# Cross-attention with 16 batches: the last 128 key columns by 15 block products in column tiles, between the steps of the product with V

## The chip, the cores and the metric

The kernel runs on one core of a Trainium2 chip. The metric is device microseconds of one execution. Three runs of the kernel before took 944.00, 943.75 and 945.24 us, median 944.0. Engines go by short names: PE is TensorE (matrix products; PEld is its weight loading), DVE is VectorE, ACT is ScalarE, POOL is GpSimd, SP is SyncE, which starts most DMA transfers. PSUM is the memory that PE writes to, in banks of 512 float32 numbers per partition; SBUF is the working memory. Everything is float32, and each product that the program issues is carried out as two passes.

## The reference, cut to what matters

```python
# x: (16, 100, 640), context: (16, 722, 384); 8 heads of 80 columns
enc, ca = context[:, :718], context[:, 718:]          # 718 keys, 4 extra tokens
hs = mha(x @ Wq, enc @ Wk, enc @ Wv)                  # softmax over the 718 keys
q1 = einsum('btc,th->bch', ca, Wq_ca)[:, picked]      # 100 of 384 rows
hs1 = mha(q1, x, x)                                   # softmax over 100 keys
hs2 = mha(hs1 @ Wq, ca @ Wk_ca, ca @ Wv_ca)           # softmax over 4 keys
out = (hs + hs2) @ Wout + b_out + x
```

There are two larger attentions per batch: the main one over 718 keys, and a second one whose own softmax is over 100 keys (with a third, tiny one behind it).

## The kernel before, in words

The 718 keys of a batch are cut into three thirds u of 240 columns (KT), two of which share a column each with a neighbour, and each third into two blocks of up to 120 (KN). So there are six key blocks. The 640 columns of K and V are cut into chunks of 128 for K (HC = 5) and two halves for V.

The products `enc @ Wk` and `enc @ Wv` are, per batch, 3 x 2 results (a third u, a half g) of a product over three context chunks. Instead of 18 block products they are formed by 15, in the manner of the fast 3x3 by 3x2 schemes: sums of context blocks (`enc_sums`, on POOL, once per batch) times sums of weight blocks (`weight_sums`, once). `V_PLAN` and `K_PLAN` list, for each of the 15, a chain (a PSUM bank A to E in which products pile up), the number of the product, and the result (u, g) to which the bank's content at that moment is added. After each product the bank is read: copied where the result is new (by ACT), else added to it by DVE. The class `Blocks` does this; `Values` is V's, `Keys` is that of the first four chunks of K.

The fifth chunk of K (columns 512 to 640) has no partner chunk, and is formed in the plain way by `last_keys`: 9 products with 128x128 weights (`wk4`) and 240 moving columns (three thirds by three context chunks), one after the other, and two copies to `kT` by ACT.

Inside the batch loop the program's order is the order on every engine: each engine works through its own queue in the order in which the kernel's text issues, and waits on semaphores where data or a buffer is not ready. For a batch b the order on PE is: the scores of b (`scores`, three pairs of key blocks), small products of the second attention (`softmax2`, `products`), V of b and the four chunks of K of b+1 in turn (`both`, lines 440 and 471), the fifth chunk of b+1 (`last_keys`, line 565), the output projection of earlier rows where a block of 128 rows is complete (`project`, line 951; in no batch 0, 1, 5, 9, 13), the queries of the next two batches where b is odd (`queries`, line 541), and the product with V of b (line 1317). That last product goes in two halves g of four heads. Each half has 24 items (head h, key block i); each item is two products with 64 and 36 of the 100 query rows as weight columns, which lie in the two column tiles of 64 of the PE array, and 81 moving columns.

On DVE the running maximum of the scores and its handling (`Maximum`) precede the subtractions from the scores (line 1144) and ACT's exponentials (line 1152). `Maximum` has five steps, taken one by one with `go(n)`: a transpose of 32x32 blocks (672), a reduction (674), four and two or four small reductions (677, 684), a spread over 800 columns (694 on ACT for the main attention, 699 on DVE for the second), and a transpose back (702). `softmax1` runs these steps for the second attention of batch b+1, then subtracts (798); `exponentials1` (801) is ACT's exponential of it. In the kernel before, for batches from 1, `softmax1` stands behind the last subtraction, as a whole, and `exponentials1` before the product with V; in batch 0 four steps stand there, and the fifth and the exponential behind the product with V. After each half of the product with V DVE normalises (reciprocal 1329, multiplication 1331, and from batch 1 the sum with the second attention, 1338).

PSUM banks come from three pools of two: `ps2` (pairs of banks: V's chains A and B, two thirds of the scores, `last_keys`, `project`), `psk` (K's chains A and B, and every other small one) and `ps1` (the other chains, `a_ps` of the product with V). A tile is handed out in rotation when its former readers are done. Remaining raw context blocks (`rest`, line of `load_rest`) are loaded into a single buffer after their last readers.

Of the kernel before, what the change touches and what calls it, by code (L numbers as in the profile page):

```python
# [75 lines left out]
def load_packed(load, to, w):  # L76
# [38 lines left out]
    ("B", 14, (0, 0)),  # L115
    ("A", 5, (1, 1)),
]

K_PLAN = [V_PLAN[k] for k in (0, 1, 2, 3, 4, 6, 5, 7, 9, 11, 8, 12, 10, 13, 14)]

# [12 lines left out]
def kernel(  # L133
# [123 lines left out]

    wv_sb = const.tile([P, NF, H // 2], F32, name="wv_sb")
    wk_sb = const.tile([P, NF, 2, P], F32, name="wk_sb")
    wk4 = const.tile([P, CC, P], F32, name="wk4")  # L260
    wq_sb = const.tile([P, HC, H], F32, name="wq_sb")
    kT = const.tile([P, HC, 3, KT], F32, name="kT")
    wout_sb = const.tile([P, HC, H], F32, name="wout_sb")
# [100 lines left out]
    e1 = const.tile([P, ROWS], F32, name="e1")  # L364
    nc.gpsimd.memset(e1[96:, :], LOW)

    ys = []
    for j in range(2):
        y = const.tile([S, NH, HT + 1], F32, name=f"y_{j}")
        nc.gpsimd.memset(y[:, :, HT:], 1.0)  # L370
        ys.append(y)


    def first_values(i, enc, engines, halves=(0, 1), get=psum):
# [215 lines left out]
    def last_keys(b, enc):  # L590
        banks = pair(f"kT_ps_{b}")
        return chunk_keys(
            HC - 1,
            [banks[:, k] for k in range(2)],
            [wk4[:, c] for c in range(CC)],
            enc,
        )


    def scores(b, g, tiles):  # L600
# [124 lines left out]
    class Second:  # L725


        def __init__(self, b, xT, ca=None):
            self.b, self.xT = b, xT[:, b % 2]
            self.top = None  # L730

            self.ca = ca
            if ca is not None:
                return
            self.ca = small.tile([S, T, S], F32, tag="ca", name=f"ca_{b}", bufs=2)
            nc.sync.dma_start(
                out=self.ca, in_=cas[b].unsqueeze(0).to_broadcast([S, T, S])
            )
# [23 lines left out]
            return summed  # L762

        def copy(self):
            b, y_ps = self.b, self.y_ps
            self.y = ys[b % 2]
            nc.scalar.copy(
                self.y[:, :, :HT].rearrange("p (u h) k -> p u h k", u=2),
                y_ps[:S, HT : 11 * HT].rearrange("p (u h k) -> p u h k", u=2, h=5)[
                    :, :, :4, :  # L770
                ],
            )
# [19 lines left out]
        def softmax1(self, n=8):  # L792

            if not self.top:
                self.top = Maximum(e1, f"1_{self.b}")
            self.top.go(n)
            if self.top.over is not None:
                nc.vector.tensor_tensor(e1[:S], e1[:S], self.top.over[:S], ALU.subtract)

        def exponentials1(self):  # L800
# [255 lines left out]
    for c in range(HC):  # L1056
        w_ps = psum(f"w_ps_{c}")
        for cc in range(CC):
            nc.tensor.transpose(
                w_ps[:, cc * P : (cc + 1) * P], wkt_sb[:, c, cc * P : (cc + 1) * P], ident  # L1060
            )
        act(
            wk_sb[:, c % 2 : 6 : 2, c // 2] if c < HC - 1 else wk4,
            w_ps[:, : CC * P].rearrange("p (a n) -> p a n", a=CC),
        )

# [15 lines left out]
        weight_sums(nc.vector, wk_sb, False)  # L1082
    first_keys(enc)
    weight_sums(nc.vector, wk_sb, True)

    va = wide("va")[:, : H // 2]
    va_ps = psum("va_ps")
# [34 lines left out]
    for b in range(B):  # L1122
# [59 lines left out]
        if b == 0:  # L1182
            second.scores1()
            m_next = load_m(b + 2)
            kk.go(3)
            top.go(3)
            first_values(3, e_in, (act, act), get=bank)
            top.go(1)
            kk.go(2)
            now.scores2()  # L1190
            first_values(0, e_in, (act, act), (0,), bank)
            top.go()
            kk.go(3)
            first_values(0, e_in, (act, act), (1,), bank)
            now.softmax3()
            kk.go(2)
            subtract(0)
            exponential(0)
            kk.go(2)
            subtract(1)  # L1200
            kk.go(3)
            exponential(1)
            second_next, enc_next = loads()
            less = subtract(2)
            exponential(2)
            last_keys(b + 1, enc)
            enc_next = load_rest(b + 2, enc_next)
            keys(m_next)
            now.values2(less)
            enc_sums(enc_next)  # L1210
            second.softmax1(4)
        elif b + 1 < B:
            if b > 1:
                last.transpose()
            vv = Values(b, e_in)

            def both(n):
                vv.go(n)
                kk.go(n)

            second.scores1(seen)
            if b == 1:
                now.load()
            last.load()
            top.go(3)
            both(3)
            now.scores2()
            top.go(1)
            both(2)
            if b == 1:  # L1230
                nc.vector.tensor_tensor(last.hs[:S], last.hs[:S], last.hs2, ALU.add)
            top.go()
            both(2)
            if b == 1:
                last.transpose(get=psum1)
            both(1)
            now.softmax3()
            now.values2()
            vv.go(2)
            kk.go(1)  # L1240
            subtract(0)
            exponential(0)
            vv.go(1)
            subtract(1)
            vv.go(1)
            kk.go(2)
            exponential(1)
            vv.go(1)
            kk.go(2)
            both(1)  # L1250
            both(1)
            if b == 1:
                for f in list(wv_there):
                    nc.scalar.copy(wv_sb[:, W_AT[f]], wv_there.pop(f))
            second.load()
            if b == 1:
                nc.gpsimd.dma_start(out=bias, in_=bout[0].partition_broadcast(P))
            second_next, enc_next = loads()
            if b + 2 < B:
                m_next = load_m(b + 2)  # L1260
            subtract(2)
            exponential(2)
            last_keys(b + 1, enc)
            if b + 2 < B:
                enc_next = load_rest(b + 2, enc_next)
            second.softmax1()
            last.project()
        else:
            room = enc_tile("spare").rearrange("p f k -> p (f k)")
            spare.extend(room[:, i * H : (i + 1) * H] for i in range(2))  # L1270
            last.transpose()
            vv = Values(b, e_in)
            last.load()
            mine.load()
            top.go(3)
            vv.go(3)
            last.project_few(len(OC) - 2)
            now.scores2()
            top.go(1)
            vv.go(2)  # L1280
            top.go()
            vv.go(3)
            now.softmax3()
            now.values2()
            vv.go(2)
            subtract(0)
            exponential(0)
            vv.go(5)
            for i in (1, 2):
                subtract(i)  # L1290
                exponential(i)
            last.project()
# [3 lines left out]
        if b % 2 and b + 1 < B:  # L1296
            xT, tiles = xT_at[0], queries_tiles(p + 1)
            for n in range(HC):
                queries(p + 1, xT, tiles, n)
        if 0 < b < B - 1:  # L1300
            second.exponentials1()

        mine.hs = hs = hs_tile(f"hs_{b}")
        hs2 = now.hs2
        for g in range(2):
            a_ps = psum1(f"a_ps_{b}_{g}")
            a_v = a_ps[:S, : 4 * (D + 1)].rearrange("p (h e) -> p h e", e=D + 1)

            order = [(h, i) for h in range(4 * g, 4 * g + 4) for i in range(len(KC))]
            if g == 0:  # L1310
                order.sort(key=lambda at: at[1] // 2)
            for h, i in order:
                if b == B - 1 and h == NH - 1 and i == 0:

                    mine.transpose([(0, 2)])
                for lo, hi in QC:
                    nc.tensor.matmul(  # L1317
                        a_v[lo:hi, h % 4],
                        st[i // 2][: KEYS[i], i % 2, h * S + lo : h * S + hi],
                        block(i, h // 4)[: KEYS[i], h % 4],  # L1320
                        start=(i == 0 and h in (0, *range(4, NH))),
                        stop=(i == len(KC) - 1),
                        skip_group_check=True,
                    )
            if b == 0 and g == 1:
                second.softmax1()
                second.exponentials1()
            rs = small.tile([S, 4], F32, tag="rs", name=f"rs_{b}_{g}")
            nc.vector.reciprocal(rs.unsqueeze(2), a_v[:, :, D : D + 1])  # L1329
            cols = slice(4 * g * D, 4 * (g + 1) * D)  # L1330
            nc.vector.tensor_tensor(
                hs[:S, cols].rearrange("p (h d) -> p h d", h=4),
                a_v[:, :, :D],
                rs.unsqueeze(2).to_broadcast([S, 4, D]),
                ALU.mult,
            )
            if b:
                nc.vector.tensor_tensor(hs[:S, cols], hs[:S, cols], hs2[:, cols], ALU.add)
# [57 lines left out]
```

## Time and profile before

| what | value |
|---|---|
| median of the runs | 944.0 us |
| profiled execution: span | 942.4 us |
| PE busy | 934.5 us (99%) |
| DVE busy | 674.0 us (72%) |
| POOL busy | 623.1 us (66%) |
| ACT busy | 364.7 us (39%) |
| product with V, line 1317 | 3072 passes, 111.9 us |
| last and first key chunks by `chunk_keys`, line 565 | 7.7% of the chain that ended last |
| DVE waiting for the product with V (line 1329) | 111.0 us in 30 waits |

The time of the profiled execution itself is known by its span, 1.6 us below the median of the runs. Busy times of engines overlap; only the chain of work that ended last adds up to the span. A line of the timeline gives the start and the duration in microseconds, the engine, the line of the kernel, the operation, the tile written and the tiles read, shapes (partitions x elements), and, in brackets, how long the engine sat idle before it and what ended that. A matmul's own duration (366 ns for a pass of 240 columns) contains the way through the array; the next pass starts earlier.

### The profile page before, as it was taken

What the parts mean: (1) busy time and instruction counts of PE and PEld (TensorE: products, weight loads), DVE (VectorE), ACT (ScalarE), POOL (GpSimd) and SP (SyncE); (2) the same over time, 40 slices, a digit from 0 to 9 for tenths busy, and PEclk for the clock granted to TensorE, in tenths of its full rate; (3) what the DMA queues carried; (4) which work ended last, traced back from release to release, by engine and by line L of the source; (5) the groups of instructions that cost most, each with busy time, mean ns of one, the idle gap of its engine ahead of it and who ended that gap; (6) DMA issues with size and microseconds to landing.
All of it is one profiled execution on the core that took longest, in us unless ns stands there. A gap on an engine that the chain in (4) does not pass through costs nothing.

```text
span 942.4 us, 25629 instructions
## 1 busy us (share of the span) xinstructions
PE 934.5 (99%) x11215; PEld 796.2 (84%) x11215; DVE 674.0 (72%) x1084; ACT 364.7 (39%) x605; POOL 623.1 (66%) x565
## 2 busy tenths in 40 slices
PE   9999999999999999999999999999999999999998
PEld 6998979888797888989789887987989888897866
DVE  3559794977929688595955959578693886949684
ACT  1244443524334244433424334244431534334241
POOL 5857976776738757495873948657694576748514
PEclk9999999999999999999999999999999999999999
DMA  8822024040310404003050130403113030210300
GB/s 264 296 60 87 3 70 128 1 130 3 94 60 1 117 2 135 5 11 122 1 151 3 37 82 1 139 1 95 38 40 113 1 112 7 59 53 1 95 8 29
DMA packets 45367, 62.48 MB, mean 66 GB/s; under 512 B 13448, under 2 KB 37320, under 8 KB 43656
## 3 DMA queue, kind: packets, MB, share of 16 engines
q1 hardware_dynamic: 41720, 42.97, 15.2%
q0 software_dynamic: 2512, 16.72, 6.1%
q8 instruction: 88, 1.44, 0.6%
q10 hardware_dynamic: 1024, 1.15, 0.4%
q14 instruction: 23, 0.19, 0.1%
HBM read 55.26 MB, written 5.57 MB: 65 GB/s over the span
## 4 chain that ended last, share of the span: by engine, by line
PE 96%; DVE 3%; issue 0%; DMA 0%; ACT 0%; POOL 0%; ACTq 0%; DVEq 0%
PE s_ps L620 12%; PE a_ps L1317 12%; PE v_psA L440 10%; PE v_psB L440 8%; PE kT_ps L565 8%; PE k_psA L471 7%; PE q_ps L541 7%; PE o_ps L951 7%; PE k_psB L471 6%; PE v_psC L440 3%; PE k_psC L471 3%; PE y_ps L746 2%; PE v_ps L381 2%; PE v_psD L440 2%; PE v_psE L440 2%; PE k_psE L471 1%
## 5 line engine op out<-in xcount | busy, mean ns | idle before, releaser
L781 POOL TENSOR_TENSOR e<-ca,g 100x800 f32<-100x800 f32 x64 | 99.8, 1570 | 145.2 <-DVE most L1156 125.0
L870 POOL TENSOR_TENSOR hs<-vb,p 100x640 f32<-100x640 f32 x64 | 105.6, 1659 | 45.9 <-DVE p L856 32.5
L877 POOL TENSOR_TENSOR hs<-hs,hs 100x640 f32<-100x640 f32 x48 | 113.9, 2373 | 3.8
L1317 PEld LDWEIGHTS a_ps<-vs,st 120*36 120x36 f32 (+3 forms) x3072 | 109.1, 125 | 5.6 <-issue 5.5
L1317 PE MATMUL a_ps<-vs,st 120*36 120x81 f32 (+3 forms) x3072 | 111.9, 233 | 0.0
L440 PE MATMUL v_psA<-wv_sb,enc 128*120 128x320 f32 x352 | 109.5, 434 | 0.0
L506 POOL TENSOR_TENSOR enc<-enc 128x240 f32<-128x240 f32 x135 | 98.1, 736 | 16.9 <-DMA enc<-in_enct 9.8
L1144 DVE TENSOR_TENSOR st<-st,over 120x1600 f32<-120x1600 f32 x48 | 107.6, 2243 | 0.0
L637 ACT COPY st<-s_ps 120x800 f32<-120x800 f32 x64 | 49.7, 829 | 135.6 <-PE s_ps L620 135.6
L620 PE MATMUL s_ps<-qp,kT 32*120 32x100 f32 x3072 | 97.4, 263 | 0.0
L620 PEld LDWEIGHTS s_ps<-qp,kT 32*120 32x120 f32 x3072 | 94.7, 179 | 1.6 <-issue 0.2
L788 POOL TENSOR_TENSOR e<-e,e 100x800 f32<-100x800 f32 x48 | 90.4, 1884 | 3.8
L440 PE MATMUL v_psB<-wv_sb,enc 128*120 128x320 f32 x296 | 91.9, 433 | 0.0
L471 PE MATMUL k_psA<-enc,wk_sb 128*128 128x240 f32 x360 | 87.6, 366 | 0.0
L1329 DVE RECIPROCAL rs<-a_ps 100x4 f32<-100x4 f32 x32 | 5.8, 182 | 111.0 <-PE a_ps L1317 111.0
L1156 DVE TENSOR_TENSOR most<-most,st 120x800 f32<-120x800 f32 x64 | 66.2, 1034 | 24.1 <-ACT st L631 23.0
L1152 ACT ACTIVATE st<-st 120x1600 f32<-120x1600 f32 x48 | 73.9, 1539 | 22.3 <-DVE st L1144 22.2
L471 PEld LDWEIGHTS k_psA<-enc,wk_sb 128*128 128x128 f32 x360 | 68.2, 190 | 16.8 <-DVE kT L411 0.2
L440 PEld LDWEIGHTS v_psA<-wv_sb,enc 128*120 128x120 f32 x352 | 63.2, 183 | 22.6 <-issue 0.5
L471 PE MATMUL k_psB<-enc,wk_sb 128*128 128x240 f32 x300 | 73.1, 366 | 0.3 <-DVE sm L853 0.3
L440 PEld LDWEIGHTS v_psB<-wv_sb,enc 128*120 128x120 f32 x296 | 54.0, 183 | 21.9 <-DVE vs L411 0.4
L541 PE MATMUL q_ps<-xT,wq_sb 128*128 128x200 f32 x400 | 69.1, 333 | 0.0
(146 smaller groups left out, 1732.8 us busy)
## 6 DMA issues: line engine op xcount, KB each, us to landing
vb<-va_d POOLq DMA_DIRECT2D x16, 1000.0 KB, 7.4
enc<-in_enct SPq DMA_DIRECT2D x30, 240.0 KB, 3.9
enc<-in_enct SPq DMA_DIRECT2D x15, 360.0 KB, 3.6
xT<-in_xt SPq DMA_DIRECT2D x8, 500.0 KB, 4.3
rest<-in_enct SPq DMA_DIRECT2D x31, 120.0 KB, 6.6
xn<-in_x SPq DMA_DIRECT2D x11, 320.0 KB, 5.7
out<-xn SPq DMA_DIRECT2D x11, 320.0 KB, 3.2
ca<-in_cas SPq DMA_DIRECT2D x16, 156.2 KB
```

What stands on the lines that cost most here:

```text
L440: nc.tensor.matmul(at[0][j][:KN, : H // 2], a_form(self.enc, f)[:, j * KN : (j + 1) * KN], wv_there.get(f, wv_sb[:, W_AT[f]]), start=first ...
L471: nc.tensor.matmul(at[:, i * KT : (i + 1) * KT], wk_sb[:, W_AT[f], i], a_form(self.enc, f), start=(first and i == 0), stop=last, skip_grou ...
L506: nc.gpsimd.tensor_tensor(out, left, right, op)
L541: nc.tensor.matmul(q_ps[:, : 2 * S].rearrange("p (j s) -> p j s", j=2), wq_sb[:, c, n * P : (n + 1) * P], xT[:, :, c, :], start=(c == 0), ...
L565: nc.tensor.matmul(bank[:, i * KT : (i + 1) * KT], weights[c], a_raw(enc, u, c), start=(i == 0 and c == 0), stop=(c == CC - 1), skip_group ...
L620: nc.tensor.matmul(s_ps[r][:n, 256 * a + lo : 256 * a + hi], kT[rows, c, u, j * KN : (j + 1) * KN], rhs, start=(a == 0 and c == 0), stop=( ...
L781: first = nc.gpsimd.tensor_tensor(to, self.ca[:, t, :].unsqueeze(1).to_broadcast([S, NH, S]), g[:, :, t].unsqueeze(2).to_broadcast([S, NH, ...
L788: nc.gpsimd.tensor_tensor(e, e, to, ALU.add)
L870: first = nc.gpsimd.tensor_tensor(to, vb[:S, t, :].rearrange("p (h d) -> p h d", h=NH), p2[:, :, t].unsqueeze(2).to_broadcast([S, NH, D]), ...
L877: nc.gpsimd.tensor_tensor(sums, sums, to, ALU.add)
L1144: return nc.vector.tensor_tensor(st[i], st[i], top.over[:KN].unsqueeze(1).to_broadcast([KN, 2, ROWS]), ALU.subtract,)
L1317: nc.tensor.matmul(a_v[lo:hi, h % 4], st[i // 2][: KEYS[i], i % 2, h * S + lo : h * S + hi], block(i, h // 4)[: KEYS[i], h % 4], start=(i ...
```

## The change

The fifth chunk of K of batch b+1 is no longer formed by 9 full products. It is formed by the same 15 block products as the others, on weight blocks of 128x64 (`wk5`, with its own sums), by a new class `LastKeys`. `REST_PLAN` puts them into eight steps: seven with two products at a time, one in partitions 0 to 63 of one PSUM bank (chains A, D and E) and one in partitions 64 to 127 of another (chains B and C), that is in the two column tiles of 64; the last step is one product, cut into two halves of 120 columns. After each step each bank's new content is read: added by DVE where the result was begun, else copied, by ACT from the first bank and by DVE from the second.

The steps are placed inside the product with V: one before the items 1, 7, 13 and 19 of each half. In batches from 1 the second attention's `softmax1` is cut: two steps of it where it stood, and one after each of the first three key steps (small reductions; spread; transpose back with the subtraction). `exponentials1` now stands behind the second half of the product with V. In batch 0 the five steps stay where they were. Apart from that, the second attention's `y` has one tile instead of two, and batch 0's first keys still go by `last_keys`, with six of `wk5`'s blocks as weights.

```diff
+REST_PLAN = [
+    (("A", 7, (2, 1)), ("B", 13, (1, 0))),
+    (("A", 3, (2, 0)), ("C", 12, (0, 1))),
+    (("A", 9, (1, 0)), ("B", 8, (2, 0))),
+    (("A", 2, (0, 0)), ("B", 10, (2, 1))),
+    (("A", 0, (0, 1)), ("B", 4, (0, 1))),
+    (("A", 5, (1, 1)), ("B", 14, (0, 0))),
+    (("D", 1, (2, 0)), ("C", 11, (2, 1))),
+    (("E", 6, (1, 0)),),
+]
+REST_COLS = {"A": 0, "B": 0, "C": KT, "D": KT}
...
-    wk4 = const.tile([P, CC, P], F32, name="wk4")
+    wk5 = const.tile([P, NF, P // 2], F32, name="wk5")
...
+    class LastKeys:
...
+        def product(self, half, f, lo, cols, keys, first):
+            nc.tensor.matmul(
+                self.banks[half][64 * half : 64 * half + 64, lo : lo + cols],
+                wk5[:, W_AT[f]],
+                a_form(self.enc, f)[:, keys : keys + cols],
+                start=first,
+                stop=True,
+                skip_group_check=True,
+            )
+
+        def read(self, half, to, lo, cols, keys):
+            u, g = to
+            out = kT[64 * g : 64 * g + 64, HC - 1, u, keys : keys + cols]
+            left = self.banks[half][64 * half : 64 * half + 64, lo : lo + cols]
+            if to in self.begun:
+                nc.vector.tensor_tensor(out, left, out, ALU.add)
+            elif half:
+                nc.vector.tensor_copy(out, left)
+            else:
+                nc.scalar.copy(out, left)
+
+        def go(self, n=1):
+            for _, step in zip(range(n), self.steps):
+                begins = self.banks is None
+                if begins:
+                    self.banks = [psumk(f"k5_ps_{self.b}_{k}") for k in range(2)]
+                if len(step) == 1:
+                    ((_, f, to),) = step
+                    for half in range(2):
+                        self.product(half, f, 0, KN, half * KN, True)
+                    for half in range(2):
+                        self.read(half, to, 0, KN, half * KN)
+                    continue
+                for half, (chain, f, _) in enumerate(step):
+                    self.product(half, f, REST_COLS[chain], KT, 0, begins)
+                for half, (chain, _, to) in enumerate(step):
+                    self.read(half, to, REST_COLS[chain], KT, 0)
+                    self.begun.add(to)
...
-            self.y = ys[b % 2]
+            self.y = y_sb
...
-            if self.top.over is not None:
+            if self.top.over is not None and not self.less:
+                self.less = True
                 nc.vector.tensor_tensor(e1[:S], e1[:S], self.top.over[:S], ALU.subtract)
...
+    weight_sums(nc.vector, wk5)
...
-            last_keys(b + 1, enc)
             enc_next = load_rest(b + 2, enc_next)
...
-            last_keys(b + 1, enc)
             if b + 2 < B:
                 enc_next = load_rest(b + 2, enc_next)
-            second.softmax1()
+            second.softmax1(2)
             last.project()
...
-        if 0 < b < B - 1:
-            second.exponentials1()
+        k5 = LastKeys(b + 1, enc) if b + 1 < B else None
...
-            for h, i in order:
+            for at, (h, i) in enumerate(order):
+                if k5 and at % 6 == 1:
+                    k5.go()
+                    if b and at < 19:
+                        second.softmax1(1)
...
-            if b == 0 and g == 1:
-                second.softmax1()
+            if k5 and g == 1:
+                if b == 0:
+                    second.softmax1()
                 second.exponentials1()
```

More of the change, by code (lines that the diff above doesn't have):

```diff
@@ L365 @@
     nc.gpsimd.memset(e1[96:, :], LOW)
[L367 to L371, printed above, removed]
+    y_sb = const.tile([S, NH, HT + 1], F32, name="y_sb")
+    nc.gpsimd.memset(y_sb[:, :, HT:], 1.0)
     def first_values(i, enc, engines, halves=(0, 1), get=psum):
@@ L594, in last_keys, with __init__ @@
             [banks[:, k] for k in range(2)],
-            [wk4[:, c] for c in range(CC)],
-            enc,
-        )
+            [
+                wk5[:, 2 * c : 2 * c + 2].rearrange("p g n -> p (g n)")
+                for c in range(CC)
+            ],
+            enc,
+        )
+    class LastKeys:
+        def __init__(self, b, enc):
+            self.b, self.enc = b, enc
+            self.banks, self.begun = None, set()
+            self.steps = iter(REST_PLAN)
+        def product(self, half, f, lo, cols, keys, first):
[34 more added lines that the diff above has]
+                    self.begun.add(to)
     def scores(b, g, tiles):
@@ L729, in __init__ @@
             self.b, self.xT = b, xT[:, b % 2]
-            self.top = None
+            self.top, self.less = None, False
             self.ca = ca
@@ L764, in copy @@
         def copy(self):
-            b, y_ps = self.b, self.y_ps
-            self.y = ys[b % 2]
+            y_ps = self.y_ps
+            self.y = y_sb
             nc.scalar.copy(
@@ L1062 @@
         act(
-            wk_sb[:, c % 2 : 6 : 2, c // 2] if c < HC - 1 else wk4,
+            wk_sb[:, c % 2 : 6 : 2, c // 2]
+            if c < HC - 1
+            else wk5[:, :6].rearrange("p (a g) n -> p a (g n)", a=CC),
             w_ps[:, : CC * P].rearrange("p (a n) -> p a n", a=CC),
```

## The prediction

> **What bounds the kernel now.** I read the page's busy shares, the granted clock and the chain of work that ended last first, because they say which engine pays for a microsecond.
>
> ```profile
> PE 934.5 (99%) x11215; PEld 796.2 (84%) x11215; DVE 674.0 (72%) x1084; ACT 364.7 (39%) x605; POOL 623.1 (66%) x565
> ...
> PEclk9999999999999999999999999999999999999999
> ...
> PE 96%; DVE 3%; issue 0%; DMA 0%; ACT 0%; POOL 0%; ACTq 0%; DVEq 0%
> ```
>
> TensorE (PE) is busy 99% of 942.4 us at a steady clock and makes 96% of the chain. So work taken from PE comes off the time, and every wait put on PE goes onto it. Next I read the chain in order of time, around one batch (b = 2, a batch with a projection).
>
> ```profile
> 195.54 3.65 PE kT_ps L565 x18
> 199.19 5.38 PE o_ps L951 x20
> 204.57 6.92 PE a_ps L1317 x191
> 211.49 7.28 PE s_ps L620 x240
> ```
>
> The last key chunk costs 3.65 us as 18 passes (each float32 product is two passes), 203 ns per pass of 240 columns. The product with V takes 6.91 us for 48 (head, key block) items, 0.144 us per item. Together 10.56 us per batch: what the change replaces.
>
> The change reads its results through VectorE (DVE), so the third view is DVE's timeline from that last chunk to the end of the product with V. Columns: start, us, engine, line, operation.
>
> ```profile
> 198.74 0.71 DVE L677 TENSOR_REDUCE side<-quad 32x25 f32<-32x25 f32 x4
> 199.48 1.30 DVE L684 TENSOR_REDUCE mx<-side 32x25 f32<-32x100 f32 x4
> 200.82 0.99 DVE L699 COPY spread<-mx 128x800 f32<-128x800 f32 x1
> 201.84 1.01 DVE L702 STREAM_TRANSPOSE over<-spread 128x800 f32<-128x800 f32 x1
> 202.89 1.00 DVE L798 TENSOR_TENSOR e<-e,over 100x800 f32<-100x800 f32 x1
> 204.67 0.82 DVE L970 TENSOR_TENSOR xn<-o_ps,xn 128x640 f32<-128x640 f32 x1 [0.77 <-POOL m L718]
> 208.16 0.18 DVE L1329 RECIPROCAL rs<-a_ps 100x4 f32<-100x4 f32 x1 [2.67 <-PE a_ps L1317]
> 208.38 0.49 DVE L1331 TENSOR_TENSOR hs<-a_ps,rs 100x320 f32<-100x320 f32 x1
> 208.98 0.69 DVE L1338 TENSOR_TENSOR hs<-hs,hs 100x320 f32<-100x320 f32 x1
> ```
>
> Today the second softmax's maximum (L677 to L798) runs beside the last key chunk and the projection, and DVE then idles through the product with V. In the changed kernel those rows stand inside that product, in one queue with the new reads. For the price of a read:
>
> ```profile
> 190.00 0.64 DVE L411 TENSOR_TENSOR kT<-k_psC,kT 128x480 f32<-128x480 f32 x1
> 190.56 0.81 DVE L411 TENSOR_TENSOR vs<-v_psA,vs 120x640 f32<-120x640 f32 x1
> 191.29 0.64 DVE L411 TENSOR_TENSOR kT<-k_psA,kT 128x480 f32<-128x480 f32 x1
> ```
>
> Independent neighbours start 0.56 us after a 480-wide add and 0.73 after a 640-wide one.
>
> **The PE work by itself.** Removed: 9 products of 240 columns, 3.65 us. Added: seven pairs and one pair of half width. Two column tiles do run side by side here: an 81-column pass alone would be 81/240 of 203 ns, 69 ns, and 192 in a row 13.2 us, but the product with V takes 6.91. So a pair costs 0.406 us, and all eight steps 7 x 0.406 + 0.203 = 3.05 us. PE gains 0.60 us per batch, 9 us in 15 batches, if nothing waits.
>
> **What waits.** Each step writes both banks, half 0 and half 1, and each half's product waits until the previous step's read of that bank is done, even where the columns differ (the changed program's waits say so: step 3's half 1 waits for the copy of step 2's half 1). The reads of half 1 are all DVE's, those of half 0 are DVE's in steps 3, 5, 7, 8 and ScalarE's in 1, 2, 4, 6. A waiting product holds everything behind it on PE, the V product too. DVE's order is: copy 1, the eight small reductions, copy 2, the spread, both adds of step 3, the transpose, the subtraction, the add of step 4, the first half's three normalising operations, both adds of step 5, and so on.
>
> Prices: a 240-wide read has no row. From 480 and 640 wide, 0.17 us per 160 columns gives 0.31 us of queue and 0.39 to its end. Its lower bound is the 0.18 of the 4-wide reciprocal, the upper the 0.64 of the 480-wide add. I take the line's value, being nearest in kind. The reductions take 2.08 (198.74 to 200.82), the spread 1.02, the transpose 1.05. The subtraction took 1.00 here with GpSimd idle and 1.40 in batch 0, at 98.08, with GpSimd adding; inside the product GpSimd forms the next batch's sums, so 1.40, with 1.00 as the other end. Normalising: 208.16 to 209.67, 1.50. A result reaches a reader 0.20 after its last pass (a record of 366 ns against 203 of streaming, and 0.04 to the reader); DVE's end reaches PE in 0.05.
>
> From the start of the product with V in b = 2, in us:
> - Step 1 at 0.14; result 0.75, but DVE has the projection's sum until 0.92 (overlap 0.08). Copy 1 from 0.84, reductions from 1.15, copy 2 from 3.23, ending 3.62.
> - Step 2 at 1.41 on time. Step 3 is due at 2.68; its half 1 waits for copy 2 until 3.67: wait 0.99.
> - Spread 3.54 to 4.56, step 3's adds end 5.26. Step 4, due 4.93, waits until 5.31: 0.38.
> - Transpose and subtraction to 7.63, step 4's add ends 8.02. Step 5, due 6.58, waits until 8.07: 1.49.
> - Normalising to 9.44, step 5's adds end 10.14. Step 6, due 9.34, waits until 10.19: 0.85.
> - Step 7 on time, step 8 waits 0.09.
>
> Sum 3.80 of waits. PE's work is 6.91 + 3.05 = 9.96, so 13.76 against 10.56: **+3.20 us**. This holds for the seven even batches from 2. Batches 3, 7, 11 end on the queries, DVE is free, copy 1 starts at 0.75: +3.11. In 1, 5, 9, 13 step 1's half 1 waits for the bank that holds the last query chunk; its two ScalarE multiplies end 0.78 after the start (150.81 + 0.74 against 150.77), so its result comes at 1.44, 0.60 later: +3.80. Batch 0 is worse: there is no projection, and copy 1 stands behind the whole maximum.
>
> ```profile
> 89.62 1.81 DVE L1144 TENSOR_TENSOR st<-st,over 120x1600 f32<-120x1600 f32 x1
> 91.36 1.00 DVE L672 STREAM_TRANSPOSE turned<-e 128x800 f32<-128x800 f32 x1
> ...
> 95.53 0.99 DVE L699 COPY spread<-mx 128x800 f32<-128x800 f32 x1
> ```
>
> PE would reach step 2 at 91.03 (start 88.83, step 1 held to 89.76 by the read of a key bank, six items); copy 1 ends at 96.52 + 0.39, so it waits 5.9 us. The rest (0.41, 41 items, five pairs, a half one, some 0.5 of waits) ends at 106.0 against 99.39: +6.6.
>
> Sum: 7 x 3.20 + 3 x 3.11 + 4 x 3.80 + 6.6 = 53.5 us.
>
> **The rest, at nothing.** ScalarE's exponential (0.87) moves behind the product with V; score copies need it out of the way only some 2.6 us later (12 us over all if that cover went). The single y tile is written after products that PE already orders before it. The load of the remaining raw keys on SP no longer waits for PE, so GpSimd's sums start sooner; they gate nothing (GpSimd waits 125 us in all for DVE's maxima). The projection takes PSUM banks last read at 193.71, before it starts. The exponential of the third score pair, which the old chunk covered, ends at 198.4; the product with V would begin at 200.9. Twelve 64-wide sums of weights before the loop, at most 0.35 us each by the 256-wide ones (7 in 2.43), at least 0.18: 2 to 4 us in DVE's gaps of 6.89 and 3.04 us there.
>
> The Trainium skill, "TensorEngine Tiling (Array Packing)", section PSUM Bottleneck, speaks against this change: tiling speeds TensorE but not the reading of PSUM, which may become the limit. By its Theoretical Speedup (2x at 64 columns) alone the sum would be the 9 us gain; by its warning, the loss above, for which it has no figure. On the clock, "TensorE: Matmul & The Clock Gate", Part 1, halves the rate after some 3.4 us of idling, for about as long. No row here has such a gap; by it batch 0's stall would add an estimated 1.7 us.
>
> **How it could go otherwise.**
> - Faster. DVE reads never hold PE: then -0.60 x 15 = -9 us, 935. It decides at step 6, which PE reaches by itself after 31 items and five pairs, 6.5 us; DVE must have read step 5 by then. DVE's queue, 0.84 to 10.14, would have to be 3.7 us shorter, more than the seven reads together. Against it: each row of that queue. Chance 0.05; within 0.2% 0.01.
> - The column tiles do not overlap. Up to step 6 PE's extra 2 us hide in the waits; steps 6 to 8 add about 0.15 + 0.41 + 0.20 = 0.76 per batch, 11 us: 1009. Against it, the 6.91 us. Chance 0.04.
> - Much smaller loss: reads at 0.18 (-0.9 per batch) and the subtraction at 1.00 (-0.4) give 53.5 - 14 x 1.3 = 35 us, 979; with waits that overlap better than by my queue, down to 965. Chance 0.12.
> - The forecast, 0.78. Upwards, reads at 0.45 of queue (towards 0.64) give 14 x 1.0 = 14 us more, 1011.
>
> **How the numbers follow.** The sum stands against the profiled execution: 942.4 + 53.5 = 995.9 us span. The median of the runs is 944.0, 1.6 above the span, so 997.5; I say 997. The range, 967 to 1012, holds the forecast and most of the smaller loss. A measurement of this kernel can tell 0.2% (2 us) from no change. Slower 0.94.
>
> **What would show it.** PE's busy share falls by several per cent, and in its list of waits the new products appear with DVE as releaser, some 3 to 4 us per batch, most at steps 3, 5 and 6; product with V and new keys together take about 13.8 us from first to last in b = 2. The copies and adds of 64x240 measure 0.3 to 0.4 us; the wait of DVE's reciprocal for PE shrinks from 111 us. I am wrong if PE runs through these steps without gaps, or if the subtraction and reductions end before the steps need DVE.

## The result: 6.9% slower, and the profile after

The changed kernel takes 1009.2 us (median of four runs, 1007.8 to 1009.8) against 944.0 (four runs). The ratio is 1.0686, 95% interval 1.0671 to 1.0701. The forecast was 997, range 967 to 1012. The profiled execution has a span of 1007.9 us against 942.4: 65.5 us more, where the sum of the prediction had 53.5.

The page of the changed kernel, engine totals, granted clock (each digit a fortieth of the span, in tenths of full clock) and the chain that ended last:

```profile
PE 967.8 (96%) x11425; PEld 796.6 (79%) x11425; DVE 740.2 (73%) x1276; ACT 374.0 (37%) x635; POOL 623.8 (62%) x564
...
PEclk9998999999999999999999999999999999999999
...
PE 81%; DVE 16%; issue 2%; DMA 1%; ACT 0%; POOL 0%; SPq 0%; ACTq 0%; DVEq 0%; POOLq 0%
```

PE made 96% of the chain before; now DVE makes 16% of it. DVE's own share of busy time rose by one point only, from 72% to 73%: an average over the span hides a queue that is full for 10.4 us on end (214.18 to 224.55 below) in each 60 or so that a batch takes.

The list of waits names the new products (line 620) as the ones held, and DVE's adds (634) and copies (636) as what released them. Columns: us in total, times, longest.

```profile
PEld k_ps L620 <- DVE kT L634: 36.6, 71, 2.3
...
PE k_ps L620 <- DVE kT L634: 18.2, 27, 1.9
...
PEld k_ps L620 <- DVE kT L636: 17.3, 15, 3.3
...
PE k_ps L620 <- DVE kT L636: 11.1, 15, 2.9
```

(A weight load and its product wait at the same time, so the PEld and PE rows are not added.) In batch 2 the projection ends at 214.11 (208.71 + 5.40) and the next scores start at 228.31, by the chain in order of time:

```profile
208.71 5.40 PE o_ps L1011 x20
...
228.31 7.28 PE s_ps L679 x240
```

That is 14.20 us for what took 10.56. DVE's timeline of the same stretch follows. L1030 is the projection's sum, 736 to 761 the maximum, 858 the subtraction, 1394 to 1403 the normalising:

```profile
214.18 0.83 DVE L1030 TENSOR_TENSOR xn<-o_ps,xn 128x640 f32<-128x640 f32 x1 [2.31 <-PE o_ps L1011]
215.04 0.41 DVE L636 COPY kT<-k_ps 64x240 f32<-64x240 f32 x1
215.37 0.70 DVE L736 TENSOR_REDUCE side<-quad 32x25 f32<-32x25 f32 x4
216.11 1.31 DVE L743 TENSOR_REDUCE mx<-side 32x25 f32<-32x100 f32 x4
217.46 0.41 DVE L636 COPY kT<-k_ps 64x240 f32<-64x240 f32 x1
217.90 0.99 DVE L758 COPY spread<-mx 128x800 f32<-128x800 f32 x1
218.91 0.84 DVE L634 TENSOR_TENSOR kT<-k_ps,kT 64x240 f32<-64x240 f32 x2
219.68 1.00 DVE L761 STREAM_TRANSPOSE over<-spread 128x800 f32<-128x800 f32 x1
220.71 1.11 DVE L858 TENSOR_TENSOR e<-e,over 100x800 f32<-100x800 f32 x1
221.85 0.41 DVE L634 TENSOR_TENSOR kT<-k_ps,kT 64x240 f32<-64x240 f32 x1
222.29 0.18 DVE L1394 RECIPROCAL rs<-a_ps 100x4 f32<-100x4 f32 x1
222.51 0.49 DVE L1396 TENSOR_TENSOR hs<-a_ps,rs 100x320 f32<-100x320 f32 x1
223.11 0.49 DVE L1403 TENSOR_TENSOR hs<-hs,hs 100x320 f32<-100x320 f32 x1
223.63 0.92 DVE L634 TENSOR_TENSOR kT<-k_ps,kT 64x240 f32<-64x240 f32 x2
```

From the first copy to the last of these adds no row is marked with idle time. PE's timeline shows where it stood still meanwhile:

```profile
217.92 0.42 PE L620 MATMUL k_ps<-enc,wk 128*64 128x240 f32 x1 [0.63 <-DVE kT L636]
...
222.32 0.42 PE L620 MATMUL k_ps<-enc,wk 128*64 128x240 f32 x1 [0.85 <-DVE kT L634]
...
224.09 0.93 PE L620 MATMUL k_ps<-enc,wk 128*64 128x240 f32 x3 [0.30 <-DVE kT L634]
```

The first resumes as copy 2 ends (217.46 + 0.41), the second as the add of step 4 ends, the third after the first add of step 5. These are steps 3, 5 and 6. The brackets count from the modelled end of the product before; PE's issue was still for longer, 1.0 and 1.2 us in the first two.

From the start of the scores to the next scores, each batch against the same batch before, in us:

| batches | forecast | measured |
|---|---|---|
| 0 | +6.6 | +8.75 |
| 1, 5, 9, 13 | +3.80 | +4.25, 4.10, 4.09, 4.20 |
| 3, 7, 11 | +3.11 | +3.27, 3.35, 3.37 |
| 2, 4, 8, 10, 12 | +3.20 | +3.66, 3.57, 3.81, 3.89, 4.27 |
| 6, 14 | +3.20 | +5.05, 5.73 |

### The profile page after: what moved, and what is told of

Same layout as the page of the kernel before. It is cut to its first block, busy times and chain, and to the rows that moved or that the text cites. A ratio compares the mean times of both kernels' runs of the same rounds, so it can differ in the third digit from the quotient of the medians.

```text
span 1007.9 us, 26292 instructions
## 1 busy us (share of the span) xinstructions
PE 967.8 (96%) x11425; PEld 796.6 (79%) x11425; DVE 740.2 (73%) x1276; ACT 374.0 (37%) x635; POOL 623.8 (62%) x564
## 4 chain that ended last, share of the span: by engine, by line
PE 81%; DVE 16%; issue 2%; DMA 1%; ACT 0%; POOL 0%; SPq 0%; ACTq 0%; DVEq 0%; POOLq 0%
PE s_ps L679 11%; PE v_psA L449 9%; PE v_psB L449 8%; PE q_ps L550 7%; PE k_psA L480 7%; PE o_ps L1011 6%; PE k_psB L480 6%; PE a_ps L1381 6%; PE v_psC L449 3%; PE k_ps L620 3%; PE k_psC L480 2%; DVE kT L634 2%; DVE mx L743 2%; PE kT_ps L574 2%; DVE e L858 2%
## 5 line engine op out<-in xcount | busy, mean ns | idle before, releaser
L1381 PE MATMUL a_ps<-vs,st 120*36 120x81 f32 (+3 forms) x3072 | 170.2, 238 | 0.0
L1381 PEld LDWEIGHTS a_ps<-vs,st 120*36 120x36 f32 (+3 forms) x3072 | 148.2, 126 | 13.7 <-issue 5.7
L620 PE MATMUL k_ps<-enc,wk 128*64 128x240 f32 x480 | 113.4, 371 | 32.5 <-DVE kT L634 18.2
L620 PEld LDWEIGHTS k_ps<-enc,wk 128*64 128x64 f32 x480 | 44.5, 137 | 60.1 <-DVE kT L634 36.6
L638 ACT COPY kT<-k_ps 64x240 f32<-64x240 f32 x60 | 21.1, 352 | 161.8 <-PE k_ps L620 161.6
L634 DVE TENSOR_TENSOR kT<-k_ps,kT 64x240 f32<-64x240 f32 (+1 forms) x150 | 57.2, 381 | 32.0 <-PE k_ps L620 23.5
```

The lines of the kernel that those rows point to most:

```text
L620: nc.tensor.matmul(self.banks[half][64 * half : 64 * half + 64, lo : lo + cols], wk5[:, W_AT[f]], a_form(self.enc, f)[:, keys : keys + col ...
L634: nc.vector.tensor_tensor(out, left, out, ALU.add)
L1381: nc.tensor.matmul(a_v[lo:hi, h % 4], st[i // 2][: KEYS[i], i % 2, h * S + lo : h * S + hi], block(i, h // 4)[: KEYS[i], h % 4], start=(i ...
```

## Experiments

The theory: PE's new steps wait for reads that stand in DVE's queue behind the second softmax's maximum and behind the normalising. Rivals: the key products are dear on PE itself; the halved clock (the 8 in the clock row) carries the loss; waits by whole bank are the cause. Every experiment is one run, except the last one with four; the four runs of the changed kernel differ by up to 2.0 us.

### No reads

```diff
                 for half, (chain, f, _) in enumerate(step):
                     self.product(half, f, REST_COLS[chain], KT, 0, begins)
-                for half, (chain, _, to) in enumerate(step):
-                    self.read(half, to, REST_COLS[chain], KT, 0)
-                    self.begun.add(to)
```

(and the same for the last step)

> Left out: the reads of the key steps' banks (copies and sums), so the last key chunk stays that of batch 0 from the second batch on. TensorE does all its work, and the second softmax's maximum stays where the change put it. Theory (TensorE waits for the reads, nothing else): the key steps then cost 3.05 us instead of 3.65 per batch, a gain of 0.6 in ten batches, a loss of 0.1 in batches 1, 5, 9, 13 for the query bank, about zero in batch 0: 939 us, with no halved clock. Rival (TensorE's own work, column tiles that do not overlap): 1009 less little; if a pair cost 0.81 instead of 0.406, 944 + 15 x 2.3 = 979.

Measured: 938.6 us. The product with V with the eight steps in it takes 9.98 us in ten batches, 10.75 in batches 1, 5, 9 and 13, and 10.86 in batch 0; the sum of passes was 9.96. The page's engine line:

```profile
PE 928.3 (99%) x11425; PEld 782.6 (84%) x11425; DVE 680.6 (73%) x1096; ACT 352.3 (38%) x575; POOL 624.3 (67%) x564
```

PE issues exactly as many passes as in the changed kernel (11425) and is busy 39.5 us less. So the column tiles do overlap and the products are cheap; the loss comes only with the reads. The maximum was still inside the product with V here, so by itself it holds nothing. This run is also the most that the idea could give: 5.4 us.

### The cut maximum alone

```diff
-            second.softmax1()
+            second.softmax1(2)
             last.project()
...
-        if 0 < b < B - 1:
-            second.exponentials1()
...
-            for h, i in order:
+            for at, (h, i) in enumerate(order):
+                if 0 < b < B - 1 and at % 6 == 1 and at < 19:
+                    second.softmax1(1)
```

(and the exponential behind the second half, as in the change; no key steps)

> The kernel before with one part of the change alone: the second softmax's maximum is cut, three of its steps and the subtraction stand inside the product with V, and the exponential behind it; the last key chunk stays nine products ahead of the projection. Theory: without key steps TensorE waits for nothing of VectorE inside the product; VectorE is free again before the first half's normalising is more than 1 us late, and nothing waits for that: 944 +- 1. Rival (the moved pieces cost time by themselves, as later exponentials or later scores): 950 or more.

Measured: 944.5 us beside 944.2; the product with V takes 6.91 or 6.92 us in every batch. The products without reads gain, and the cut maximum without key steps costs nothing: the loss needs reads that stand in a queue with other work.

### The maximum whole, ahead of the projection

```diff
-            second.softmax1(2)
+            second.softmax1()
             last.project()
...
                     k5.go()
-                    if b and at < 19:
-                        second.softmax1(1)
```

> The second softmax's maximum is put back whole to where it stood before the change, ahead of the projection and the queries; the eight key steps stay inside the product with V. Theory (VectorE's queue between the reads holds TensorE): in the odd batches VectorE has finished the maximum before the product with V starts, so their loss falls from 3.3 to 4.3 us each to about 0.3 (3, 7, 11) and 1.0 (1, 5, 9, 13: the query bank); in the even batches the maximum ends only some 3 us after the product starts, so the wait moves to step 2 and they keep about 3 us each; batch 0 keeps its 8.7. Together about 979 us. Rival (the key products themselves are dear on TensorE, by column tiles that do not overlap or by restarts): no change, 1009. Rival (the halved clock carries the loss): only batches 0 and 14 would change, at most 3 us, 1006.

Measured: 992.8 us. Batches 3, 7 and 11 lose 0.9 to 1.0 us instead of 3.3, batches 1, 5, 9 and 13 1.5 instead of 4.1 to 4.3. The even ones stay at 3.6 to 5.3: DVE is still in the maximum when the product starts, and step 2 stands 2.7 us. So the pattern by kind of batch, which neither rival has, came as expected, though the sum did not (979 expected): the odd batches kept 0.5 to 0.7 us more than expected, and the even ones between 0.6 and 2.3 more. In batch 3 PE's only long wait left is step 6:

```profile
286.09 0.93 PE L620 MATMUL k_ps<-enc,wk 128*64 128x240 f32 x3 [0.43 <-DVE kT L634]
```

### The normalising later as well

```diff
+            halves_v.append(a_v)
+            if k5 and g == 0:
+                continue
+            for k in range(2) if k5 else (g,):
+                rs = small.tile([S, 4], F32, tag="rs", name=f"rs_{b}_{k}")
+                nc.vector.reciprocal(rs.unsqueeze(2), halves_v[k][:, :, D : D + 1])
...
```

(the maximum whole, ahead; both halves' reciprocals and multiplications behind the second half)

> As the run with the maximum whole ahead of the projection, and both halves of the product with V are normalised behind the second half, after the last key step's sums. Theory (VectorE's queue): in that run batch 3 kept every step on time but step 6, whose half 1 waited from 6.6 to 7.9 us behind the first half's normalising; that wait of 0.8 us and its restart go in all batches with steps: 1.09 + 14 x 0.85 = 12 us less than that run's 992.8, so 980.5. Batches 3, 7 and 11 come to about +0.1 us against the kernel before. Rival (step 6 waits for its own reads, not for the normalising): 992.

Measured: 981.3 us. In batch 3 the product with the steps takes 10.50 us instead of 11.51, and step 6 starts 6.54 us after the product instead of 7.36. Batches 3, 7 and 11 come to -0.05 to -0.15 us against the kernel before. Step 6 now starts with no idle time in front of it:

```profile
281.76 0.37 PE L620 MATMUL k_ps<-enc,wk 128*64 128x240 f32 x1
```

Step 6's wait was the normalising. Batches 5, 9 and 13 still lose 0.48 us and the even ones from 2 on 2.9 to 4.3, where step 2 waits for the maximum as before.

### The maximum behind the product with V, twice

First, three steps and the subtraction ahead of the second half's normalising:

```diff
                     k5.go()
-                    if b and at < 19:
-                        second.softmax1(1)
...
             if k5 and g == 1:
-                if b == 0:
-                    second.softmax1()
+                second.softmax1()
                 second.exponentials1()
             rs = small.tile([S, 4], F32, tag="rs", name=f"rs_{b}_{g}")
```

> The last three steps of the second softmax's maximum, and its subtraction, stand behind the second half of the product with V, as they do for batch 0's fifth step; the eight key steps stay inside the product. Theory (VectorE's queue): the waits at steps 3, 4 and 5 go, the one at step 6 behind the normalising stays at about 0.9 us; a batch costs 0.3 us more than before the change, 1.0 in batches 1, 5, 9, 13, and batch 0 keeps 8.7: about 960 us, if the moved pieces hold nothing in the scores that follow. Rival (TensorE's own work): 1009. Rival (clock): not below 1004.

Measured: 1035.8 us, the worst of all: the expectation missed by 76 us, in the one place it left open. From the product's start to the scores it is as forecast, 11.5 to 11.9 us, and 12.3 in batches 1, 5, 9 and 13 (12.7 in batch 14). But from the scores to the second attention's next products it takes 10.6 to 13.7 instead of 7.28. The wait list of this kernel names the place:

```profile
PE s_ps L679 <- DVE hs L1393: 40.2, 14, 2.9
```

The second pair of scores takes the banks of the product with V, and those are released by the normalising, which now stood behind 5 us of maximum. The halved clock added to it: in nine stretches of this run, some 48 us in all, PE had half its clock, which by estimate (half of that time lost at most) is up to 24 of the 92 us.

Second, the same with the maximum behind the normalising too (the cut is against the run before):

```diff
-            if k5 and g == 1:
-                second.softmax1()
-                second.exponentials1()
             rs = small.tile([S, 4], F32, tag="rs", name=f"rs_{b}_{g}")
...
+            if k5 and g == 1:
+                second.softmax1()
...
+        if b:
+            now.exponentials1()
         st.append(scores(b, 2, tiles))
```

> As the run with three steps of the maximum behind the product with V, but those steps now follow the second half's normalising too, and ScalarE's exponential of the second softmax stands between the second and the third pair of the next scores. Theory (the loss of that run was scores waiting for the product's banks, held by a normalising that stood behind 5 us of maximum, with the halved clock on top): the scores run through in 7.3 us plus at most 1 us for the later exponential; from the product's start to the scores stay 11.5 us, 12.3 in batches 1, 5, 9, 13: 8.4 + 10 x 0.95 + 4 x 1.7 + 14 x 0.6 = 33 us over the kernel before, 977. Rival (the maximum itself, wherever it stands, costs TensorE its 5 us): 1009 or more.

Measured: 975.6 us. Scores to the next products 7.56 us, product to scores 11.5 to 12.5. Where in the queue the 5 us of maximum stand, not that they are done, decides: the kernels of 1035.8, 1009.2, 992.8 and 975.6 us differ in nothing else but the place of the maximum and of its exponential, and in what the clock did in consequence.

### Four banks

```diff
-                self.banks[half][64 * half : 64 * half + 64, lo : lo + cols],
+                self.banks[half + 2 * (lo > 0)][64 * half : 64 * half + 64, lo : lo + cols],
```

(and the same in the reads, with two more banks, each begun by its first product)

> The changed kernel with chains C and D in two banks of their own, so that step 3's half 1 (chain B) waits only for step 1's copy and no longer for step 2's, which touches other columns. Theory (VectorE's queue is what the steps wait for; which step waits matters little): the 1.0 us before step 3 goes, but step 4 still waits for step 3's sums, which stand behind the same copies, reductions and spread, until about 5.8 us, and all later waits stay: 14.0 to 14.2 us from the product's start to the scores in batch 2, 1006 to 1009 in all. Rival (the waits by whole bank, for columns that are not touched, are the cost): 1.0 us less in each of 14 batches, 995.

Measured: 1005.6 us. Step 3 of batch 2 now starts both halves on time (2.69 us after the product instead of 2.70 and 3.90); step 4 waits until 5.36 and 5.80 us, as in the changed kernel (5.35 and 5.79). Batch 3 takes 13.85 instead of 13.92 us; batch 2 takes 14.58, more than expected, with its second sum (one of the normalising operations) stretched to 1.03 us. Of the 4.1 us between the spans 3.1 are batch 0's, whose second step no longer waits for the copy behind the whole maximum; its clock is also half for 3.4 us only, where it was 6.8. So the wait by whole bank only chose the step at which PE stood; in batch 0 it did cost.

### Batch 0 by the plain products

```diff
             exponential(2)
+            last_keys(b + 1, enc)
             enc_next = load_rest(b + 2, enc_next)
             keys(m_next)
...
-        k5 = LastKeys(b + 1, enc) if b + 1 < B else None
+        k5 = LastKeys(b + 1, enc) if 0 < b < B - 1 else None
```

(Three of the weight blocks that these products use hold sums by then, so batch 1's last key chunk has other values; sizes and order are those of the kernel before.)

> Batch 0 alone goes back to the nine plain products; all other batches as in the changed kernel. Theory: batch 0's 8.75 us go, with the halved clock behind its long wait: 1000.5 us; the other fourteen batches lose what they lost. If batch 0's loss were carried over from something the change does before the loop, it would stay: 1009.

Measured: 999.8 us; batch 0 at -0.23 us, the others at 55.5 us together instead of 56.6. Single batches up to 12 moved by up to 0.7 us either way, and batch 14, whose clock is not halved here, by 1.7. The clock is full throughout, so the halved clock does not carry the loss. In the changed kernel, windows of batch 0 show it halved (columns: window, length, busy us and instructions of each engine, clock, DMA):

```profile
95.00:97.00 2.00, 0.08 (x2) 0.08 (x4) 1.79 (x4) 0.00 (x0) 1.84 (x2) 0.50 0.00 0
97.00:99.00 2.00, 2.00 (x25) 1.78 (x27) 0.41 (x1) 0.00 (x0) 1.92 (x2) 0.50 0.00 0
...
101.50:104.00 2.50, 2.50 (x59) 2.42 (x55) 1.47 (x4) 0.35 (x1) 2.42 (x5) 1.00 0.03 7
```

With PE fully busy in both, 2.0 us at half clock carried 25 passes, and 2.5 us at full clock 59.

### GpSimd out of the way

The first attempt issued GpSimd's sums behind the product in the kernel's text:

```diff
-        if 0 < b < B - 2:
-            keys(m_next)
-            enc_sums(enc_next)
...
+        if 0 < b < B - 2:
+            keys(m_next)
+            enc_sums(enc_next)
         mine.hs2 = hs2
```

> The changed kernel with GpSimd's products for the next second attention and its thirteen sums of context blocks issued behind the product with V (in its own queue, after the product's instructions), so that GpSimd is free during the key steps. Theory (GpSimd's work beside VectorE's subtraction and second sum stretches them, 1.19 us on average against 1.00 and 0.54 against 0.49, most in batch 6 with 1.52 and 1.04): they fall to 1.00 and 0.49 and TensorE gets the difference, some 3 to 5 us: 1005. If GpSimd waits for nothing that the product orders, its sums start as early as before and nothing changes: 1009. Rival (its later sums hold the next batch's products): slower than 1009.

Measured: 1010.9 us. GpSimd has nothing else in its queue there, so its order was the same, and the run is in effect a repeat of the changed kernel. As that it tells something: here batch 6 loses 3.56 us (5.05 in the changed kernel) and batch 8 loses 4.62 (3.81), with a subtraction of 1.50 us and a second sum of 1.05 in batch 8. Which of the even batches up to 12 is hit differs from run to run; batch 14, at 5.74, was hit again. The second made the first of these instructions wait for the multiplication of the second half:

```diff
+            if behind and c == 0:
+                wait_for(made, behind)
...
-            keys(m_next)
+            keys(m_next, scaled)
             enc_sums(enc_next)
```

> The changed kernel with GpSimd's products for the next second attention and its thirteen sums made to wait for the second half's normalising, so that GpSimd is free of them during the key steps (the projection's bias sums stay). Theory (the spread between batches of one kind is GpSimd's work beside VectorE's operations on SBUF: 0.99 us for the subtraction in seven batches against 1.09 to 1.52 in six others, and 1.04 against 0.49 for the sum in batch 6): the subtraction comes to 0.99 in batches 1 to 13, batch 6 falls from +5.05 to about +3.7, together 3 us less: 1006. Rival (the spread has another cause): the same spread, 1009. If GpSimd's later sums hold the next batch's products: slower.

Measured: 1004.7 us, and the spread is gone: the even batches from 2 lose 3.47 to 3.51 us, all but batch 6 (4.45); 3, 7 and 11 lose 3.24 to 3.35; 1, 5, 9 and 13 lose 4.01 to 4.05. DVE's subtraction and second sum, first in the changed kernel, then in this one:

```profile
L858 DVE TENSOR_TENSOR e<-e,over 100x800 f32<-100x800 f32 x16 | 19.1, 1192 | 0.5
...
L1403 DVE TENSOR_TENSOR hs<-hs,hs 100x320 f32<-100x320 f32 x30 | 16.1, 536 | 2.1
```

```profile
L860 DVE TENSOR_TENSOR e<-e,over 100x800 f32<-100x800 f32 x16 | 16.1, 1006 | 0.6
L1402 DVE TENSOR_TENSOR hs<-hs,hs 100x320 f32<-100x320 f32 x30 | 15.1, 503 | 2.1
```

Batch 6's remaining 0.9 us lies ahead of the product with V: from the product's start to the scores it takes 14.10 us, as the other even ones do (14.09 to 14.10). What holds it there was not traced further.

### A version with the best of it

Even batches form the chunk ahead of the projection by plain weight blocks, odd ones by the steps, with the maximum whole ahead, the normalising behind, and in batches 1, 5, 9 and 13 each step four items later:

```diff
+            if b % 2 == 0:
+                last_keys(b + 1, enc)
...
+        k5 = LastKeys(b + 1, enc) if b % 2 and b + 1 < B else None
+        first_step = 5 if b % 4 == 1 else 1
...
-                if k5 and at % 6 == 1:
+                if k5 and at % 6 == first_step:
```

> The attempt at a better version: even batches form the last key chunk ahead of the projection by products with the plain weight blocks (in column tiles, from kept copies); odd batches, where the queries give VectorE time to finish the maximum first, have the key steps inside the product with V, normalising behind it, and in batches 1, 5, 9 and 13 each step four items later, past the query bank's last reader. Theory: even batches +0.0, odd ones between -0.6 (no wait at all) and +0.3 (two reads of 0.43 us in steps 3, 5 and 7 overrun the 0.86 us to the next step by some 0.2): 940 to 946, most likely 943. Rival (the key steps are dear by themselves): 944 + 7 x 1 = 951.

Measured: 948.7 us, above the 940 to 946 expected; ratio 1.0054, interval 1.0036 to 1.0072; its four runs lie between 946.4 and 950.0, its profiled span is 944.7. In the profile, batches 3, 7, 9, 11 and 13 are 0.06 to 0.15 us better than before, but the even ones from 2 on 0.30 to 0.37 worse, batch 1 by 0.40 and batch 5 by 0.16. In the even ones the chunk is formed in pairs of column tiles, not by the old 128-wide weights. In batch 2, 0.14 of the 0.37 us lie between the chunk's first pass and the projection's (3.79 us, 3.65 before), the rest before and after; why was not tested. That three of the timed runs lie above the profiled one is not fully explained; the mean granted clock of the two slowest was 0.998, of the others 1.000. Nothing here beats the kernel before.

## Why the prediction was right

**The direction and the mechanism** held step by step, and the signs named ahead appeared: the new products wait for DVE, and DVE's reciprocals wait 10.6 us for PE where they waited 111.0. Forecast and measured starts of the two halves in batch 2, after the product's start:

| step | due | forecast | measured |
|---|---|---|---|
| 3, half 1 | 2.7 | 3.67 | 3.90 |
| 4, half 1 | 4.9 | 5.31 | 5.79 |
| 5, half 1 | 6.6 | 8.07 | 8.30 |
| 6, half 1 | 9.3 | 10.19 | 10.58 |
| scores | 9.96 without waits | 13.76 | 14.22 |

("due" of a step as the forecast had it, after the waits before.) PE's own 9.96 us were 9.98 in the run without reads. The rival "column tiles do not overlap" is gone with that run, and so is "reads never hold PE".

**The price of a read was too low.** The prediction took 0.31 us of queue and 0.39 to the end. Measured: 0.41 for a lone copy or add, 0.84 to 0.92 for two adds in a row (0.3 to 0.4 each had been named as the sign). From one start to the next in the rows above, the seven reads take 0.33, 0.44, 0.77 for two, 0.44 and 0.92 for two, 2.90 us where 2.25 were reckoned. Copy 1 also starts 1.02 us in instead of 0.84, since it did not overlap the projection's sum.

**The subtraction was priced too high for most batches.** 1.40 us with GpSimd beside it was a row of the trace; in seven of the fourteen batches it took 0.99 and in the others 1.09 to 2.19. Normalising took 1.34 instead of 1.50. Start +0.18, reads +0.65, subtraction (0.26) and normalising (0.16) less, give +0.41 for step 6, where 0.39 was measured. That two terms were too low and two too high, and half cancelled, is luck.

**What the sum lacked** is 12.0 us: 5.3 us in twelve batches together (these terms, and GpSimd's stretching, above all in batch 12); 1.85 in batch 6 (subtraction 1.52, second sum 1.04 us; 0.44 of it ahead of the product with V); 2.5 in batch 14, where the subtraction took 2.19 us beside GpSimd's bias sums and the clock then fell to half for 3.4 us; 2.15 in batch 0; and 0.16 ahead of the loop. In batch 0 the long wait came where it was forecast (step 2's half 1 at 96.92, as copy 1 ends; the forecast had 96.9), but the clock was half from 94.44 to 101.26 us. The prediction had the Trainium skill's rule on the clock, "TensorE: Matmul & The Clock Gate", Part 1, in a sentence outside its sum, with 1.7 us for batch 0. The run agrees with it in that a stall halved the clock, but not in the lengths: the clock fell at 94.44 us, when PE had stood 2.27 us, run two passes and stopped again, and it stayed half for 6.8 us, not for about 3.4. An estimate for it belonged in the sum. With these 12 us the result lies near the upper end of the range: that end came from dearer reads (1011), not from the clock or from GpSimd.

**What was costed at nothing** stayed there: the scores after the product take 7.27 to 7.28 us to the second attention's products in all batches but 0 (7.34, as before) and 1 (7.70, behind batch 0's late maximum), so elsewhere the moved exponential held nothing; the loop starts 0.16 us later than before, with twelve more sums ahead of it. The warning of the Trainium skill, "TensorEngine Tiling (Array Packing)", PSUM Bottleneck, that tiling does not speed the reading of PSUM and that this may become the limit, agrees with the run without reads (938.6 us against 1009.2). But the reads are the smaller part of the queue that holds PE: in batch 2 the seven up to step 5 take 2.90 us from start to start, and the maximum, the subtraction and the normalising 6.6.

## What to carry to other kernels

Before work is put into an engine's queue between two instructions that the busiest engine waits for, add up that queue from the first read to the last, not the share of busy time: DVE stood at 72% and was full in this stretch. A gap in which DVE waits for PE is only free while nothing that PE issues waits for DVE. And when a piece is moved out of the way, look at what is behind it at its new place: with the same 5 us of maximum the kernel lost 92 us where they stood ahead of a normalising that releases banks, and 32 us where they stood behind it, the clock's part included.

## What was not expected of the hardware

Single waits of some 2 us can be followed by half the clock. In batch 14 of the changed kernel the longest wait is 1.93 us:

```profile
950.46 0.42 PE L620 MATMUL k_ps<-enc,wk 128*64 128x240 f32 x1 [1.93 <-DVE kT L634]
```

The clock is half from 951.18, after PE had resumed, until 954.60. In the run with the maximum ahead of the projection, step 2 stands about 2.7 us in each even batch, and in batches 2, 8 and 12 a halved stretch of 3.41 us follows, in 4, 6, 10 and 14 none; the former lose 5.2 to 5.3 us, the latter 3.6 to 4.1. With the normalising later too it was five of the seven. The halved stretches last 3.41 or 6.83 us, and batches that differ in nothing else of note so differ by 1.2 to 1.7 us. The rule of the Trainium skill, "TensorE: Matmul & The Clock Gate", Part 1, speaks of an idle window of about 3.4 us; by the brackets no wait of PE at a halved stretch of these runs was longer than 2.9 us, and the measurement decides.

The length of the wait alone does not decide: in the run with the maximum ahead of the projection batch 2's wait of 2.35 us (by the bracket) was followed by a halved stretch, batch 4's of 2.52 was not. The place in time bears on it. In one run the halved stretches begin whole multiples of 3.413 us apart (there at 93.90, 216.78, 575.18 and 814.11 us: 36, 141 and 211 steps after the first). Cut into steps of 3.413 us from there, the step before each of the three has PE busy for 1.06 to 1.23 us; the emptiest one of batches 4, 6, 10 and 14 has 1.59 or more. So it seems to count how little PE did in one step of a fixed grid. No run here measures the limit: in the run with the maximum behind the product with V, 1.65 us of busy time were followed by a halved stretch too.

After a wait, the passes of a held product follow each other at 0.25 us instead of 0.20, and the two halves of a pair run one after the other: step 4 of batch 2 has its passes at 5.35, 5.60, 5.79 and 6.04 us, where an unheld step 1 has 0.17, 0.19, 0.38 and 0.40. A held pair takes 0.9 us instead of 0.4.
